# Layer 0 of a four-layer convolution network: the output scales as a row on every partition, made by a matrix product

## The chip, the cores and the metric

The kernel runs on one core of a Trainium2 chip. The time is the device time of one execution in microseconds (us). The kernel before took 5655.76 us, the median of three runs (5650.31, 5659.83 and 5655.76). The engines of the core are named as the profile names them: PE (matrix products; PEld is its weight load), DVE (VectorE), ACT (ScalarE), POOL (GpSimd) and SP, whose queue issues the transfers (DMA).

## What is computed

Input x has 32 images of 96 channels and 56 x 56 points. Four layers follow one another, each with a group normalisation in front and a sum with its input behind. Layer 0 is an inverted bottleneck with 576 inner channels:

```python
def _bn(x, g, b, m, v):
    scale = g / jnp.sqrt(v + EPS)                     # EPS = 0.001
    return x * scale[:, None, None] + (b - m * scale)[:, None, None]
identity = x
h = jnp.einsum('nchw,oc->nohw', x, w_exp)             # 96 -> 576
h = jax.nn.silu(_bn(h, g1, b1, m1, v1))
h = depthwise_3x3(h, w_dw)
h = jax.nn.silu(_bn(h, g2, b2, m2, v2))
s = h.mean(axis=(2, 3))
s = jax.nn.silu(s @ w_se1.T + b_se1)
s = jax.nn.sigmoid(s @ w_se2.T + b_se2)
h = h * s[:, :, None, None]
h = jnp.einsum('nchw,oc->nohw', h, w_proj)            # 576 -> 96
h = _bn(h, g3, b3, m3, v3)
return h + identity
```

(`depthwise_3x3` stands for the reference's grouped convolution.) Layer 1 is a wavelet convolution, layer 2 a quantised bottleneck, layer 3 a 9 x 9 depthwise convolution with kernels computed from `diff_metric`. Only the last normalisation of layer 0, with g3 and v3, is touched here: its 96 scales are folded into the projection weights.

## The kernel before

Layer 0 holds channels on partitions and takes one image after another. The order of the PE, DVE and ACT instructions of an image is written out by hand in `L0_ORDER`; the steps of image 0 up to its normalised input are in `FIRST = "s u m q v w b n"` and run ahead, outside the pipeline: s sums the image on ACT, u averages over channel groups on PE, m makes the mean on DVE, q and v do the same for squares, w (`deviation`, L393 and L395) makes the deviation on DVE and its power -1/2 on POOL, b (`norm_bias`, L399 to L403) the bias on DVE, n (`normalise`, L408) writes `xn` on ACT. Everything that PE does in layer 0 starts from `xn`.

Ahead of `FIRST` stand loads and small work on weights, whose order is the scheduler's:

- SP issues all loads in one queue (L278, L88, L268 and so on). The image comes first.
- `wproj` (128 partitions x 5 blocks x 96 outputs) is multiplied by the 96 output scales, which must lie as a row on each of the 128 partitions (L296 to L302). They are computed there: g3 and v3 are loaded as rows to all partitions (`out_rows`, at first room inside `h2s[0]`), POOL adds EPS (L299) and raises 128 x 96 values to -1/2 (L300), DVE multiplies by g3 (L301) and multiplies `wproj` by the row (L302).
- The scales of the other two normalisations (`sc`, `bi`, L315 to L328) have channels on partitions: POOL raises 128 x 5 and 128 x 11 values (L321). `both3` (`sc3`, `bi3`, L329 to L335) holds the same 96 output scales a second time, as a column: one value on each of 96 partitions (L332).
- `filt` (L344) spreads the depthwise taps over 32 x 32 unit matrices `eye4`, 3072 values on each partition, by one DVE multiplication. PE uses it as the weights of `psd` (L493).
- `brief` hands out short-lived room inside `h2s[1]`.

After `FIRST` the call `tables` makes the filter tables of layers 1 and 3: `diffusion_kernels` (L1385 to L1406; two powers of 96 x 81 values on POOL, L1402 and L1403, held back until the deviation of image 0 is issued), `wavelet_filters` (L643 to L694; small DVE work and many DVE copies into `zt`, L693) and `diffusion_filters` (L1415 to L1425; POOL copies `rev` and `zt`, then the transfer `zdiff`). Behind `tables` the pool `l0l` takes over the memory of the tables; it holds `hc`, `wg`, `hab` and one `h2` image. So `hc` (first written at L460 by ACT) has to wait until the tables are stored, `zdiff` last. The depthwise taps that run on DVE are L467 (`tap`), each reading the padded image and its own sum, both in SBUF.

`psum` of layer 0 has three buffers of the tag `mm`, taken in turn by all products of the expansion, filter and projection.

Of the kernel before, what the change touches and what calls it, by code (L numbers as in the profile page):

```python
# [10 lines left out]
F32 = mybir.dt.float32  # L11
# [4 lines left out]
ALU = mybir.AluOpType  # L16
# [4 lines left out]
B, C, H, W = 32, 96, 56, 56  # L21
# [19 lines left out]
EPS_L0 = 1e-3  # L41
# [199 lines left out]
def layer0(ctx, tc, S, x, w, y0, tables, aside, keep):  # L241
# [10 lines left out]
    nc = tc.nc  # L252
# [3 lines left out]
    psum = ctx.enter_context(tc.tile_pool(name="l0p", bufs=3, space=PSUM))  # L256
# [5 lines left out]
    ND = NBLK  # L262
    GC = 32
    HALF = 64

    def load(name, shape):
        t = cp.tile(shape, F32, tag=name, name=name)
        nc.sync.dma_start(t, w[name])  # L268
        return t
# [22 lines left out]
    wproj = load("l0_wproj", [128, ND, C])  # L292
    out4 = load("l0_out", [C, 4])

    h2s = [cp.tile([128, H, W], F32, tag=f"h2{i}", name=f"h2{i}") for i in range(2)]
    out_rows = h2s[0].rearrange("p h w -> p (h w)")[:, : 2 * C].rearrange("p (n c) -> p n c", n=2)  # L296
    nc.sync.dma_start(out_rows, w["l0_out_rows"].to_broadcast([128, 2, C]))
    gain = out_rows[:, 1]
    nc.gpsimd.tensor_scalar(gain, gain, EPS_L0, None, ALU.add)  # L299
    nc.gpsimd.tensor_tensor(gain, gain, S.mhalf[:, 0:1].to_broadcast([128, C]), ALU.pow)  # L300
    nc.vector.tensor_tensor(gain, gain, out_rows[:, 0], ALU.mult)  # L301
    nc.vector.tensor_tensor(wproj, wproj, gain.unsqueeze(1).to_broadcast([128, ND, C]), ALU.mult)  # L302
    room, at = h2s[1].rearrange("p h w -> p (h w)"), [0]

    def brief(*shape):

        n = math.prod(shape)
        at[0] += n
        t = room[:, at[0] - n : at[0]]
        return t if len(shape) == 1 else t.rearrange("p (a b) -> p a b", b=shape[1])  # L310
# [5 lines left out]
    for j in range(2):  # L316
        g, b_, m, v = ((mid1, mid2)[j][:, i, :] for i in range(4))
        n = (DV + NG, ND)[j]
# [3 lines left out]
        s = cp.tile([128, n], F32, tag=f"s{j}", name=f"s{j}")  # L322
# [7 lines left out]
    sc3, bi3 = both3[:, 0:1], both3[:, 1:2]  # L330
# [8 lines left out]
    planes = [cp.tile([128, HH, W2], F32, tag=f"plane{g}", name=f"plane{g}") for g in range(NG)]  # L339
    mv_all = cp.tile([C, B, 2], F32, tag="mv0", name="mv0")  # L340

    eye4 = brief(GC)
    nc.sync.dma_start(eye4, w["eye4"])
    nc.vector.tensor_tensor(filt, eye4.unsqueeze(1).to_broadcast([128, NG * NM, GC]),  # L344
                            wphase.rearrange("p g n -> p (g n)").unsqueeze(2).to_broadcast([128, NG * NM, GC]), ALU.mult)

# [2 lines left out]
    def image(b):  # L349

        if b not in ims:
            pair, xt = xs.pop(b)
            ims[b] = {
                "b": b, "pair": pair, "xt": xt, "h2": [None] * DV, "ps": [None] * NP, "pad": hpad, "added": set(),
                "ss": sm.tile([128, ND], F32, tag="ss", name="ss"),
            }
        return ims[b]


    small = psm.tile([128, 8, 8], F32, tag="small", name="small")  # L360
    pn = psm.tile([128, 2, B], F32, tag="pn", name="pn")
    spare = pairs[0].rearrange("c r i q -> c (r i q)")
    stats = spare[:, 3 * B : 3 * B + 12 * NP].rearrange("c (a b) -> c a b", b=6)
    later = []
# [245 lines left out]

    with tc.manual_schedule(engines=MANUAL):
        for s in FIRST.split():
            step[s](image(0))
    tables(ims[0]["pow"].ins)
    late = ctx.enter_context(tc.tile_pool(name="l0l", bufs=1))
# [895 lines left out]
def kernel_body(tc, w, x, out):  # L1511
    nc = tc.nc
    with ExitStack() as ctx:
# [29 lines left out]
        def keep():  # L1543
            pool = ctx.enter_context(tc.tile_pool(name="kept", bufs=1, side="right"))
            row = pool.tile([128, 2 * B + 1], F32, tag="row", name="row")
            return pool.tile([128, H * NPH, 2, W4], F32, tag="kept", name="kept"), row

        kept, row, left, made = layer0(tc, S, x, w, y0, tables,
               [lambda c=c: wavelet_matrices(nc, z1, z2, z3, t1, t2, t3, c) for c in range(C)]
               + [lambda c=c: matrix_rows(nc, td[c], zd[c], 1) for c in range(C)], keep)  # L1550
# [54 lines left out]
def layouts(a):  # L1605
# [25 lines left out]
    def halved(v):  # L1631

        c = v[256:320]
        return np.stack([v[:128], v[128:256], np.concatenate([c, c]), v[320:448], v[448:]], axis=1)
# [5 lines left out]
    def phase_taps(v):  # L1640
# [15 lines left out]
    i0, i2 = "L0_conv_", "L2_conv_"  # L1656
# [11 lines left out]
        "l0_wse1": halved(a[i0 + "w_se1"].T),  # L1668
        "l0_bse1": a[i0 + "b_se1"].reshape(SEH, 1),
        "l0_wproj": halved(a[i0 + "w_proj"].T),  # L1670
        "l0_out_rows": np.stack([a[i0 + "g3"], a[i0 + "v3"]])[None],
        "l0_out": np.stack([a[i0 + n] for n in ("g3", "b3", "m3", "v3")], axis=1),
        "l1_base": np.concatenate(
            [np.pad(a["L1_conv_base_w"].reshape(C, 5, 5)[:, ::-1], ((0, 0), (1, 1), (1, 1))).reshape(C, 49),
# [43 lines left out]
```

## Time and profile before

The profiled execution took 5647.33 us; the span of its instructions, to which all times of the trace refer, is 5645.5 us, so 1.8 us lie around it.

| what | value |
|---|---|
| median of three runs | 5655.76 us |
| profiled execution | 5647.33 us |
| its span | 5645.5 us |
| mean granted PE clock | 0.987 |
| PE, DVE, ACT, POOL busy from 0 to 24 us | 0.62, 0.62, 9.24, 16.56 us |
| the same from 24 to 44 us | 0.34, 5.53, 0.00, 15.51 us |
| the same from 44 to 101 us | 39.79, 48.43, 33.32, 49.51 us |
| PE busy from 242 to 800 us | 558.00 of 558 us |

The page gives busy time by engine, 40 slices of the span with a digit for each, and the chain of waits: the work that ended last, followed back from its end, each step to what released it. The timeline gives each instruction with its start and its length. An instruction's length can reach past the start of the next one on its engine; the distance between two starts is what it costs the queue.

### The profile page before, as it was taken

To read this page: it belongs to the slowest core of one execution; us is meant where nothing else is said; L and a number is where in the kernel's file an instruction comes from. 1 tells how busy PE (TensorE), PEld (TensorE's weight loads), DVE (VectorE), ACT (ScalarE), POOL (GpSimd) and SP (SyncE) were. 2 spreads that over 40 slices of the span, in tenths; PEclk is the share of its full clock that TensorE was granted. 3 is DMA by queue.
4 is the path that set the end of the run, shared out by engine and by line. 5 is a ranking of instruction groups with operands and counts; after the bars stand their busy time and mean duration, and the time that the engine had idled before them with its cause. 6 is when DMAs were issued, how large, how long until landed. Compare 5 with 4: busy or idle time off the path is not lost.

```text
span 5645.5 us, 137543 instructions
## 1 busy us (share of the span) xinstructions
PE 5420.9 (96%) x59704; PEld 3086.1 (55%) x59704; DVE 4691.7 (83%) x5413; ACT 4179.3 (74%) x6072; POOL 240.3 (4%) x161
## 2 busy tenths in 40 slices
PE   5999999999999999998899999999999999999999
PEld 2333333333333333333666666788878777787444
DVE  6999999999999999997777776777777777676777
ACT  5888888888888888885666664777777777676455
POOL 6000000000000000000000000000000000000000
PEclk9999999999999999998999999999999999999999
DMA  3023333322233232214577776479688697763888
GB/s 100 15 56 64 58 59 56 59 46 52 54 60 62 55 56 53 49 32 38 151 156 160 160 161 128 21 51 54 44 53 46 49 53 41 49 51 41 240 249 249
DMA packets 1289849, 456.13 MB, mean 81 GB/s; under 512 B 1104211, under 2 KB 1285187, under 8 KB 1287323
## 3 DMA queue, kind: packets, MB, share of 16 engines
q1 hardware_dynamic: 1289243, 447.32, 51.1%
q8 instruction: 469, 7.68, 0.6%
q14 instruction: 137, 1.12, 0.1%
HBM read 285.41 MB, written 214.08 MB: 88 GB/s over the span
## 4 chain that ended last, share of the span: by engine, by line
PE 82%; ACT 5%; DVE 5%; DMA 4%; issue 2%; SPq 1%; POOL 1%; ACTq 0%; DVEq 0%; POOLq 0%
PE psd L493 18%; PE psd L1294 13%; PE psj L548 11%; PE ps L426 8%; PE ps L1275 7%; PE pse L449 6%; PE pc L935 5%; PE pc L1469 4%; PE psj L1337 4%; DMA X<-y 2%; ACT hi L1245 2%; PE pc L923 1%; PE pa L897 1%; ACT u L1265 1%; DVE xl L884 1%
## 5 line engine op out<-in xcount | busy, mean ns | idle before, releaser
L467 DVE SCALAR_TENSOR_TENSOR h<-hpad,l_wdw,h 128x3136 f32<-128x3136 f32 x512 | 1782.2, 3481 | 9.1
L493 PE MATMUL psd<-plane,filt 128*32 128x392 f32 (+5 forms) x16384 | 1084.1, 485 | 0.6 <-issue 0.6
L1294 PE MATMUL psd<-apad,diag 64*64 64x392 bf16 x20736 | 914.5, 330 | 54.0 <-issue 50.1
L1294 PEld LDWEIGHTS <-diag 64*64 64x64 bf16 x20736 | 700.9, 106 | 262.8 <-issue 97.0
L493 PEld LDWEIGHTS psd<-plane,filt 128*32 128x32 f32 (+1 forms) x16384 | 389.5, 108 | 676.3 <-issue 623.5
L1265 ACT ACTIVATE u<-ps,o,s 128x784 int16<-128x784 f32 x576 | 537.4, 1003 | 164.9 <-PE ps L1275 145.9
L1265 ACT ACTIVATE a<-psd,o,s 128x784 int16<-128x784 f32 x448 | 424.6, 1002 | 263.3 <-PE psd L1294 263.2
L748 ACT COPY T<-raw 128x112 f32<-128x112 f32 (+2 forms) x1386 | 445.9, 385 | 230.0 <-DMA raw<-tdiff 170.3
L426 PE MATMUL ps<-xn,l_wboth 96*128 96x392 f32 (+1 forms) x1536 | 465.9, 506 | 23.9 <-ACT xn L408 23.2
L467 DVE SCALAR_TENSOR_TENSOR hc<-hhalf,l_wdw,hc 128x1568 f32<-128x1568 f32 x256 | 473.7, 1850 | 16.2 <-ACT hc L460 9.5
L1275 PE MATMUL ps<-hi,l_w1q 96*128 96x392 f32 x1280 | 464.0, 363 | 6.7 <-DVE u L1263 3.8
L935 PE MATMUL pc<-x,T 128*112 128x416 f32 (+1 forms) x1152 | 451.6, 529 | 6.1 <-DVE x L873 6.1
L1275 PE MATMUL ps<-lo,l_w1q 96*128 96x392 f32 x1280 | 439.2, 343 | 2.9 <-DVE lo L1253 2.9
L1469 PE MATMUL pc<-x,T 128*112 128x416 f32 (+1 forms) x1152 | 417.1, 523 | 13.8 <-ACT T L748 7.7
L449 PE MATMUL pse<-xn,l_wboth 96*32 96x392 f32 x4096 | 392.3, 501 | 4.5 <-ACT hab L470 4.5
L426 PEld LDWEIGHTS ps<-xn,l_wboth 96*128 96x128 f32 (+1 forms) x1536 | 219.4, 173 | 249.2 <-issue 54.5
L470 ACT ACTIVATE hab<-psd,o,s 128x784 f32<-128x784 f32 x256 | 283.7, 1113 | 59.5 <-PE psd L493 57.3
L1469 PEld LDWEIGHTS pc<-x,T 128*112 128x112 f32 x1152 | 203.2, 177 | 227.2 <-issue 188.7
L436 ACT ACTIVATE hpad<-ps,o,s 128x784 f32<-128x784 f32 x256 | 278.5, 1104 | 50.1 <-PE ps L426 48.8
L548 PE MATMUL psj<-h,wg 128*32 128x392 f32 x3072 | 306.4, 514 | 0.1
L548 PE MATMUL psj<-hab,wg 128*32 128x392 f32 x3072 | 304.8, 510 | 0.0
L935 PEld LDWEIGHTS pc<-x,T 128*112 128x112 f32 x1152 | 193.6, 180 | 154.9 <-issue 154.9
(267 smaller groups left out, 7684.8 us busy)
## 6 DMA issues: line engine op xcount, KB each, us to landing
X<-y SPq DMA_DIRECT2D x192, 392.0 KB
y<-xt SPq DMA_DIRECT2D x108, 392.0 KB
y<-y SPq DMA_DIRECT2D x96, 392.0 KB
out_dram<-y SPq DMA_DIRECT2D x96, 392.0 KB
twav<-zwav SPq DMA_DIRECT2D x768, 36.8 KB
y<-kept SPq DMA_DIRECT2D x72, 392.0 KB
xt<-y SPq DMA_DIRECT2D x59, 392.0 KB
xt<-in_x_dram SPq DMA_DIRECT2D x8, 2352.0 KB
```

The costliest lines, as they stand in the source:

```text
L426: nc.tensor.matmul(ps[p, j, :NT], wexp[:, k * 128 : k * 128 + 128][:, m], im["xn"][:, j, rows, :].rearrange("c h w -> c (h w)"), start=Tru ...
L449: nc.tensor.matmul(ps[f * GC : (f + 1) * GC, half, :NT].rearrange("p (r w) -> p r w", w=W2), wexp[:, c : c + GC], im["xn"][:, f % 2, r0 : ...
L467: nc.vector.scalar_tensor_tensor(h2, taken(im, k, t), wdw[:, k, t : t + 1], h2, ALU.mult, ALU.add)
L470: nc.scalar.activation(view, ps, AF.Silu, bias=bi[1][:, c : c + 1], scale=sc[1][:, c : c + 1], accum_out=accum)
L493: nc.tensor.matmul(ps[at * GC : (at + 1) * GC, r, :NT].rearrange("p (r w) -> p r w", w=W2)[:, r0 - half * n : r1 - half * n, q0:q1], filt[ ...
L548: nc.tensor.matmul(ps[s * GC : (s + 1) * GC, t, :NT].rearrange("c (m r q) -> c r q m", m=2, q=W4), wg[p, k, c * GC : (c + 1) * GC], phases ...
L748: nc.scalar.copy(to.rearrange("x t (p s) -> x t p s", p=NPH), v[:, k])
L935: nc.tensor.matmul(ps[:PH, to], st["T"][j][:, h, k, :], st["x"][:, j, h, of], start=first and n == 0, stop=not first and n == NK - 1)
L1265: nc.scalar.activation(out, ps, AF.Identity, bias=o[:, c : c + 1], scale=s[:, c : c + 1])
L1275: nc.tensor.matmul(ps[:, j, :NT], w1[:, k * 128 : k * 128 + 128], im[part][:, r0 : r0 + RT, :].rearrange("c h w -> c (h w)"), start=(part ...
L1294: nc.tensor.matmul(ps[q, j, :NT].rearrange("p (r w) -> p r w", w=W), diag[p, k, t, :], v, start=(t == 0), stop=(t == 8))
L1469: nc.tensor.matmul(ps[:, :, to], st["T"][:, h, k, :], st["x"][:, h, :, of], start=(n == 0), stop=(n == NK - 1))
```

## The change

The row of scales is no longer computed on 128 partitions. It is made out of the column `sc3`, which the kernel computes anyway: `each3` is `sc3` copied along 128 columns (96 x 128), `eye3` is a 96 x 96 unit matrix put together from `eye4`, and the product of the two on PE has the 96 scales as a row on each of 128 partitions. DVE multiplies `wproj` by it out of PSUM. That product and the multiplication are called between the steps b and n of `FIRST`.

```diff
-    out_rows = h2s[0].rearrange("p h w -> p (h w)")[:, : 2 * C].rearrange("p (n c) -> p n c", n=2)
-    nc.sync.dma_start(out_rows, w["l0_out_rows"].to_broadcast([128, 2, C]))
-    gain = out_rows[:, 1]
-    nc.gpsimd.tensor_scalar(gain, gain, EPS_L0, None, ALU.add)
-    nc.gpsimd.tensor_tensor(gain, gain, S.mhalf[:, 0:1].to_broadcast([128, C]), ALU.pow)
-    nc.vector.tensor_tensor(gain, gain, out_rows[:, 0], ALU.mult)
-    nc.vector.tensor_tensor(wproj, wproj, gain.unsqueeze(1).to_broadcast([128, ND, C]), ALU.mult)
...
-    eye4 = brief(GC)
+    eye4, eye3, each3 = brief(GC), brief(C)[:C], brief(128)[:C]
     nc.sync.dma_start(eye4, w["eye4"])
+    nc.vector.memset(eye3, 0.0)
+    for i in range(C // GC):
+        at = slice(i * GC, (i + 1) * GC)
+        nc.vector.tensor_copy(eye3[at, at], eye4[at])
+    nc.vector.tensor_copy(each3, sc3.to_broadcast([C, 128]))
     nc.vector.tensor_tensor(filt, eye4.unsqueeze(1).to_broadcast([128, NG * NM, GC]),
...
+    def scaled_weights():
+        gain = psum.tile([128, 2, 512], F32, tag="mm", name="psg")[:, 0, :C]
+        nc.tensor.matmul(gain, each3, eye3, start=True, stop=True)
+        nc.vector.tensor_tensor(wproj, wproj, gain.unsqueeze(1).to_broadcast([128, ND, C]), ALU.mult)
...
         for s in FIRST.split():
+            if s == "n":
+                scaled_weights()
             step[s](image(0))
...
-        "l0_out_rows": np.stack([a[i0 + "g3"], a[i0 + "v3"]])[None],
```

## Prediction

> **What bounds the kernel now.** I read the page's busy table and slices first, then the chain of waits for the first 110 us, then the timelines of DVE and POOL there.
>
> ```profile
> PE 5420.9 (96%) x59704; PEld 3086.1 (55%) x59704; DVE 4691.7 (83%) x5413; ACT 4179.3 (74%) x6072; POOL 240.3 (4%) x161
> PE   5999999999999999998899999999999999999999
> POOL 6000000000000000000000000000000000000000
> ```
>
> PE fills nearly every slice of 141 us but the first, and the first is the only one in which POOL works for long. So the kernel as a whole is PE's; what this change can touch is how late PE gets going. The chain says what that hangs on (start, length, what):
>
> ```profile
> 15.49 3.37 DMA h<-in_l_out_rows_dram
> 18.93 0.47 POOL h L299
> 19.59 0.23 POOL h L320
> 19.82 1.17 POOL h L321
> 20.99 15.61 POOL h L300
> 36.60 2.08 POOL h L321
> 38.69 0.51 POOL both L332
> 39.20 4.45 issue
> 43.68 0.56 POOL rstd L395
> ...
> 89.02 6.32 POOL zt L1424 x16
> 95.35 5.78 DMA zdiff<-zt
> 101.24 1.61 ACT hc L460
> ```
>
> The power of the row, L300, lies on the chain with 15.6 us; the small powers that everybody needs queue behind it. What the chain calls issue is filled in by the timeline:
>
> ```profile
> 38.88 0.65 DVE L302 TENSOR_TENSOR l_wproj<-l_wproj,h 128x480 f32<-128x480 f32 x1
> 39.75 3.35 DVE L344 TENSOR_TENSOR filt<-h 128x3072 f32<-128x3072 f32 x1
> 43.09 0.15 DVE L384 TENSOR_REDUCE ts<-small 96x1 f32<-96x4 f32 x1
> 44.45 3.98 ACT L408 ACTIVATE xn<-xt,nb,rstd 96x784 f32<-96x784 f32 x4 [20.65 <-DVE nb L399]
> ```
>
> PE's second group sum, which L384 waits for, is done by 24.3 us: nothing but DVE's queue (the multiplication of wproj and filt, held by POOL's powers) keeps xn from starting. From the deviation (rstd, 43.68) on, POOL goes through the tables until 95.35, zdiff is stored until 101.2, and hc, PE's filters and the pipeline follow. From 242 to 800 us PE is busy for 558 of 558 us: a shift of its start should reach the end.
>
> **The change, part by part.** Costs in a queue are distances between starts.
>
> *The load of out_rows (96 KB) goes.* SP issues one every 0.47 us, so the loads behind it, mid1, wphase, eye4 and the tables', go out 0.47 us earlier. POOL waited for out_rows until 18.93; in the changed order it waits next for mid1 (22 KB), issued in that place at 15.49. Not later than 18.93, then; earlier by at most the 74 KB less at the 110 GB/s that flowed there (0.67 us). I take 18.6.
>
> *POOL.* L299 (0.43) and L300 (15.60) go. Left are the sums on mid1 (0.24) and sc3 (0.19), then the powers of 5 columns (1.18), 11 (2.08) and 1 (0.55): 18.6 + 0.43 = 19.03, 20.21, 22.29, 22.84. Before, the last ended at 39.20. The row costs 0.16 us a column, the same in L300 (96 columns, 15.64) and L1402 (81 columns, 13.80). Here the Trainium skill speaks against the change: GPSIMD Engine Reference, § 4.1 Engine selection, has POOL about twice as slow as DVE in two-input elementwise work. DVE multiplies the same 128 x 96 values in 0.26 us (L301), so by the rule L300 would be 0.5 us and the change would bring nothing. The row decides: this operation is a power, and the trace has it at thirty times the rule's price.
>
> *DVE ahead of filt.* L301 goes (beside POOL, on no path of its own); L302 leaves this place (0.57). After both3 at 22.9 the order has six small ones at 0.075 (0.45), three copies of 32 x 32 (unseen; by the copies of 96 x 25 into G at 0.08 to 0.09: 0.27; bounds 0.2 and 0.5) and the copy to 96 x 128 (unseen; between the 96 x 81 and 96 x 162 rows, 0.11 and 0.23: 0.2). filt starts at 23.85. The memset of eye3 comes first in DVE's queue, which is idle until 19.1: nothing; without that cover some 0.2. eye4 and wphase have long landed, as DMA is idle from 21 us on.
>
> *From filt to xn.* filt still holds the queue for 3.27 us: L384 at 27.1. That is what is late next; PE's sum has lain ready since 24.3. Then 0.52 (0.59 less L335, which no longer stands between) to the power of the deviation at 27.65, and 0.77 as before to xn at **28.4 in place of 44.45: 16.0 us earlier**.
>
> *The product psg.* Its weights and its 96 x 96 stream are like the group sums' (0.4 and 0.3 us) and fall into PE's idle time between 24.3 and 31. If that cover were gone, 0.7 us.
>
> *wproj out of PSUM* stands behind b1 and ahead of the diffusion chain's z in DVE's queue. Price 0.57 as L302: PSUM adds nothing, since L567 with one PSUM input takes 555 ns for 392 values and L302 652 ns for 480. Waiting behind it: the z chain, hence POOL's table powers, and the zt copies. They are **15.5 us earlier, not 16.0**. psg takes one of three mm buffers, so the third pair of expansion products waits for this multiplication; that is over near 29.5, and PE needs the buffer 2.6 us after its first product, near 34.
>
> *POOL's tables.* Do they keep pace? Each copy to rev lies in one of two classes:
>
> ```profile
> L1415 POOL COPY rev<-yy x9: 187/189/3649, 75.2 to 86.2; 96x9 f32<-96x9 f32 x9
> 75.72 14.03 DVE L467 SCALAR_TENSOR_TENSOR h<-hpad,l_wdw,h 128x3136 f32<-128x3136 f32 x4
> 89.92 3.48 DVE L467 SCALAR_TENSOR_TENSOR h<-hpad,l_wdw,h 128x3136 f32<-128x3136 f32 x1
> ```
>
> Median 189 ns, but up to 3649: as long as a DVE tap. A copy is held until the tap beside it ends. The same page of the skill (§ 8 Key points) has POOL contending with DVE instructions that read two SBUF inputs, which the taps do. So POOL's end follows DVE's last tap (93.4) and some ten free copies of 0.2, and what counts is whether DVE's taps keep pace. In the changed order the first two taps stand a little ahead of the third set of filter sums. The first waits for ACT's h, which ends at 60.46 - 16.0 = 44.4, and DVE gets there at about 44.25. That wait is 0.2 us, DVE's work is the same, and the tables move by 15.5. Lower bound of the shift 14.5 (a few copies held again), upper 16.5.
>
> *Behind it.* zdiff, then hc at 85.7 in place of 101.24. PE's gap before its filters (4.46 us at 106.7) grows by the half us that xn gained more. PE's granted clock was 0.50 from 105.3 to 112.2 there. The skill (TensorE: Matmul & The Clock Gate, Part 1) lets the clock fall and rise by windows of about 3.4 us that don't start with the kernel. By the row I would copy the half-speed time unchanged; by the rule it may differ by a window, 1.7 us of time either way. I take the row, the rule widens the range.
>
> **Sum.** -15.5 us (-13 to -17.5). Against the profiled execution: 5647.33 - 15.5 = 5631.8. That execution was 8.4 us below the median of the three runs; from the median, **5640.3**.
>
> **Rivals.**
>
> *The gain is taken back later (5655.8).* A transfer or table chain that doesn't start with xn would have to set layer 0's end. For it: the loads at the start do have fixed times, and DVE is 97% busy in layer 0 (541.5 of 558 us). Against: DMA share is 0.00 from 24 to 44 us, so all loads are in, and the later transfers stand in SP's queue behind zwav and zdiff, which move too. DVE's taps also begin earlier.
>
> *Slower.* One place: DVE's first tap, now ahead of the third set of filter sums. DVE takes its queue in order, so a wait W there delays the zt copies, the later taps, POOL's held copies, zdiff and hc by W. It decides from W = 15.5 and shows as slower from W = 26.8 (5667). The timeline gives ACT's h at 60.46, one us before the tap of the old place; W near 27 would need h behind all of ACT's expansions, and it is ACT's fifth piece of work after the table load.
>
> That the change doesn't do what it says is out: the new order has no power of 96 columns, and PE's and ACT's orders differ by psg alone.
>
> **How the numbers follow.** The forecast has 0.82, the gain taken back 0.13, slower 0.05. The forecast's own range is 5634 to 5647: the shift's bounds and the runs' scatter of 4 to 5 us about the median. A measurement of this kernel can tell about 0.2%, 11.3 us, from no change; 15.5 is not far beyond it, and about one in eight of the first case would read as the same. So faster 0.72; same 0.10 + 0.13 = 0.23; slower 0.05. The range reaches towards the second case: 5632 to 5652.
>
> **What would show it.** POOL without L300 and its last small power ending near 22.8; filt starting near 23.9 and xn near 28.4; psg in PE's idle time; the zdiff transfer issued near 79.8 (95.35 before) and hc near 85.7; from there the same rows, 15.5 us earlier, to a span near 5630. Wrong if xn starts early but hc stays where it was (POOL or zdiff bound by something else), if hc moves but the span doesn't, or if the first tap waits for many us.

## Result and profile after

The kernel after took 5639.6 us (median of 14 runs, 5626.5 to 5656.4), the kernel before, on the same chip, 5652.3 us (median of 14 runs, 5642.3 to 5666.6): a ratio of 0.9973, 95% interval 0.9963 to 0.9983. The profiled execution took 5626.9 us, its span 5625.0 us against 5645.5.

The page of the kernel after, busy table and slices:

```profile
PE 5413.7 (96%) x59706; PEld 3072.7 (55%) x59706; DVE 4693.5 (83%) x5417; ACT 4177.4 (74%) x6072; POOL 226.9 (4%) x159
PE   6999999999999999998899998999999999999999
POOL 5000000000000000000000000000000000000000
```

PE's first slice rises from 5 to 6 tenths and POOL's falls from 6 to 5: apart from one late slice of PE that reads 8 for 9, these two rows differ in the first 141 us alone. The chain of waits of the kernel after, first 110 us (start, length, what):

```profile
15.39 2.19 DMA h<-in_l_mid_dram
17.66 0.26 POOL h L313
...
18.10 3.26 POOL h L314 x2
21.36 0.51 POOL both L325
21.88 4.94 issue
26.85 0.56 POOL rstd L399
...
43.40 16.70 POOL z L1409
60.17 2.75 POOL z L1411
63.00 3.36 POOL yy L1412
66.43 10.83 POOL rev L1421 x9
...
79.87 2.54 POOL zt L1430 x16
82.43 5.77 DMA zdiff<-zt
88.38 1.61 ACT hc L464
```

The 15.6 us of the row's power are gone and the small powers end at 21.88 (39.20 before). The deviation comes at 26.85 (43.68), and `xn` starts at 27.62 in place of 44.45: 16.83 us earlier. But `hc` starts at 88.38 in place of 101.24: 12.86 us earlier. Some 4 us were lost in between, and they sit on this chain as POOL's work on the tables. The rows of the same three operations, first from the POOL timeline of the kernel before, then of the kernel after (start, length, line):

```profile
60.29 13.31 POOL L1403 TENSOR_TENSOR z<-z,yy 96x81 f32<-96x81 f32 x1
73.69 1.01 POOL L1405 TENSOR_SCALAR z<-z 96x81 f32<-96x81 f32 x1
74.79 0.35 POOL L1406 TENSOR_TENSOR yy<-z,yy 96x81 f32<-96x81 f32 x1
```

```profile
43.40 16.68 POOL L1409 TENSOR_TENSOR z<-z,yy 96x81 f32<-96x81 f32 x1
60.17 2.74 POOL L1411 TENSOR_SCALAR z<-z 96x81 f32<-96x81 f32 x1
63.00 3.36 POOL L1412 TENSOR_TENSOR yy<-z,yy 96x81 f32<-96x81 f32 x1
```

The second table power took 3.37 us longer, the two small operations behind it 1.73 and 3.01 us. What stood beside them is in the DVE timeline of the kernel after:

```profile
43.44 3.47 DVE L471 SCALAR_TENSOR_TENSOR h<-hpad,l_wdw,h 128x3136 f32<-128x3136 f32 x1
...
59.16 14.03 DVE L471 SCALAR_TENSOR_TENSOR h<-hpad,l_wdw,h 128x3136 f32<-128x3136 f32 x4
...
73.36 3.47 DVE L471 SCALAR_TENSOR_TENSOR h<-hpad,l_wdw,h 128x3136 f32<-128x3136 f32 x1
90.01 3.74 DVE L471 SCALAR_TENSOR_TENSOR hc<-hhalf,l_wdw,hc 128x1568 f32<-128x1568 f32 x2 [13.19 <-ACT hc L464]
```

The first depthwise tap of image 0, which in this order stands ahead of the third set of filter sums, starts at 43.44: 0.04 us after the second power. Before, it started at 61.53, 1.24 us after it. The power grew by about one tap's length. Follow the advance over the kernel before along POOL: 16.9 us where the second power starts, 13.5 behind it, 11.8 and 8.8 behind the two small operations, 9.2 at the copies into `zt`. Those copies then take 2.53 us and not 6.31, because DVE's last tap is over at 76.8 and they run beside nothing: 12.9 at the store of `zdiff`. DVE itself sits idle for 13.19 us until `hc` comes.

### The profile page after: what moved, and what is told of

Read it like the earlier page. It is cut to its first block, busy times and chain, and to the rows that moved or that the text cites. A ratio compares the mean times of both kernels' runs of the same rounds, so it can differ in the third digit from the quotient of the medians.

```text
span 5625.0 us, 137545 instructions
## 1 busy us (share of the span) xinstructions
PE 5413.7 (96%) x59706; PEld 3072.7 (55%) x59706; DVE 4693.5 (83%) x5417; ACT 4177.4 (74%) x6072; POOL 226.9 (4%) x159
## 4 chain that ended last, share of the span: by engine, by line
PE 76%; DMA 8%; ACT 6%; DVE 5%; SPq 2%; issue 2%; POOL 1%; ACTq 0%; DVEq 0%; POOLq 0%
PE psd L497 18%; PE psd L1300 13%; PE psj L552 11%; PE ps L430 8%; PE ps L1281 7%; PE pse L453 6%; PE pc L941 4%; PE psj L1343 3%; DMA X<-y 3%; ACT hi L1251 2%; ACT u L1271 2%; PE pc L1475 1%; PE pc L929 1%; DMA raw<-tdiff 1%; DVE h L471 1%
## 5 line engine op out<-in xcount | busy, mean ns | idle before, releaser
L471 DVE SCALAR_TENSOR_TENSOR hc<-hhalf,l_wdw,hc 128x1568 f32<-128x1568 f32 x256 | 473.7, 1850 | 19.9 <-ACT hc L464 13.2
L1475 PE MATMUL pc<-x,T 128*112 128x416 f32 (+1 forms) x1152 | 418.6, 524 | 14.0 <-ACT T L754 11.8
```

The source lines that it names most:

```text
L471: nc.vector.scalar_tensor_tensor(h2, taken(im, k, t), wdw[:, k, t : t + 1], h2, ALU.mult, ALU.add)
L1475: nc.tensor.matmul(ps[:, :, to], st["T"][:, h, k, :], st["x"][:, h, :, of], start=(n == 0), stop=(n == NK - 1))
```

## Experiments

The theory after this reading: the early `xn` is worth about 16.5 us, and the tap's new place gives some 4 back, since a POOL instruction that starts beside a tap is held until the tap ends. Rivals: the gain comes from less work, so that a row power moved elsewhere on POOL would cost its 16 us still; the lost 4 us belong to something other than the tap's place. Each of the first four kernels ran beside the same kernel before (median of 67 runs 5649.5 us), the last three beside another set (median of 46 runs 5647.7 us).

**The power put back, with its result unused.** The kernel after, plus the load, EPS and the power of 96 columns in their old places; the scales still come from the product.

```diff
+    out_rows = h2s[0].rearrange("p h w -> p (h w)")[:, : 2 * C].rearrange("p (n c) -> p n c", n=2)
+    nc.sync.dma_start(out_rows, w["l0_out_rows"].to_broadcast([128, 2, C]))
+    gain = out_rows[:, 1]
+    nc.gpsimd.tensor_scalar(gain, gain, EPS_L0, None, ALU.add)
+    nc.gpsimd.tensor_tensor(gain, gain, S.mhalf[:, 0:1].to_broadcast([128, C]), ALU.pow)
```

> The changed kernel, with the load of the rows, their EPS and their power of 128 x 96 on GpSimd put back in the old place; their result is not used, the scales still come from the product. Theory (the power stands in GpSimd's queue ahead of the small powers, and all else hangs on those): the normalised input of image 0 starts near 44.4 us again, hc near 101 to 104, ratio to the kernel before 1.000 within 0.001. Rival (the gain comes from what else changed: VectorE's two multiplications ahead of filt, their order, the product on the idle TensorE): the normalised input stays below 30 us and the ratio near 0.997.

Measured: 5649.5 us, ratio 0.9999 (0.9985 to 1.0012). `xn` starts at 44.5, as expected, and `hc` at 105.2, beyond the expected 101 to 104. POOL timeline of this kernel, then a row of its DVE timeline:

```profile
20.62 15.63 POOL L300 TENSOR_TENSOR h<-h,mhalf 128x96 f32<-128x96 f32 x1
...
60.32 16.68 POOL L1414 TENSOR_TENSOR z<-z,yy 96x81 f32<-96x81 f32 x1
```

```profile
60.36 3.47 DVE L476 SCALAR_TENSOR_TENSOR h<-hpad,l_wdw,h 128x3136 f32<-128x3136 f32 x1
```

The whole gain goes with work on POOL whose result nobody reads: `xn` is 16.9 us later than in the kernel after, 15.6 of them the power and 1.3 the load and the EPS sum that came back with it. And the run isolates the loss: `xn` stands where it stood before, the second power starts where it started before (60.32 against 60.29), but takes 16.68 us, with the first tap at 60.36; `hc` is 4.0 us later than before. That is the price of the new order alone. The 16.8 us of early `xn` less these 4.0 make the 12.9 of the kernel after, to within 0.1 us.

**The power kept, but late.** The kernel before, with the row's power behind image 1's deviation on POOL, and `wproj` multiplied where image 0's gated weights are made; no product.

```diff
+        if im["b"] == 1:
+            with tc.issue_after(im["pow"].ins):
+                nc.gpsimd.tensor_scalar(wg[:, 1], wg[:, 1], EPS_L0, None, ALU.add)
+                nc.gpsimd.tensor_tensor(wg[:, 1], wg[:, 1], S.mhalf[:, 0:1].to_broadcast([128, C]), ALU.pow)
...
+        if im["b"] == 0:
+            nc.vector.tensor_tensor(wg[:, 1], wg[:, 1], wg[:, 0], ALU.mult)
+            nc.vector.tensor_tensor(wproj, wproj, wg[:, 1].unsqueeze(1).to_broadcast([128, ND, C]), ALU.mult)
```

> The kernel before, with the row still made by GpSimd's power of 128 x 96, but issued behind the deviation of image 1, and multiplied into wproj just ahead of the first gated weights; no product on TensorE. Theory (only the place in GpSimd's queue mattered): normalised input near 26.9 us, hc near 85, layer 0 some 16 us ahead, ratio 0.997. Rival (the power has to be removed, since GpSimd's 16 us come back as a wait of image 1 or of the first projection): the normalised input as early, but layer 0 by its end less than 6 us ahead, ratio above 0.999.

Measured: 5630.8 us, ratio 0.9974 (0.9964 to 0.9984); `xn` at 27.1, `hc` at 84.0. POOL timeline of this kernel:

```profile
42.48 13.29 POOL L1404 TENSOR_TENSOR z<-z,yy 96x81 f32<-96x81 f32 x1
...
104.41 18.82 POOL L392 TENSOR_TENSOR wg<-wg,mhalf 128x96 f32<-128x96 f32 x1
```

The power is even longer here, 18.82 us beside DVE's taps (it starts 0.17 us behind the start of one, at 104.24), and costs the kernel nothing: it ends at 123.2, and its result is read at 140.8. So it was never the amount of POOL's work, only its place ahead of the small powers: the first rival is out. The old order of the taps leaves the second power at 13.29 us, and `hc` gains 17.3, all that `xn` gained.

**The first tap behind the third filter set.** The kernel after, with one order mended on DVE (`MARK["g"]` is the last copy into `G`).

```diff
+        if "g" in MARK:
+            with tc.issue_after(MARK.pop("g").ins):
+                nc.vector.scalar_tensor_tensor(h2, taken(im, k, t), wdw[:, k, t : t + 1], h2, ALU.mult, ALU.add)
+            return
...
-                nc.vector.tensor_copy(g, F[:, abs(da), abs(dp)])
+                MARK["g"] = nc.vector.tensor_copy(g, F[:, abs(da), abs(dp)])
```

> The changed kernel, with VectorE's first depthwise tap put behind the third set of filter sums again, as in the kernel before. Theory (in the changed kernel the tap started 0.04 us after the second table power and held it for its whole length): the second power takes 13.3 us in place of 16.7, GpSimd's tables end near 79 us in place of 82.4, hc starts near 85 in place of 88.4, the end some 3.4 us earlier than the changed kernel's. Rival (the tables are held by taps in any order because the taps came forward by more than the tables): second power or the pieces behind it held as long, tables end within 1 us of 82.4.

Measured: 5629.7 us, ratio 0.997 (0.996 to 0.998). POOL timeline of this kernel, then the first tap from its DVE timeline:

```profile
43.66 13.29 POOL L1416 TENSOR_TENSOR z<-z,yy 96x81 f32<-96x81 f32 x1
57.04 1.51 POOL L1418 TENSOR_SCALAR z<-z 96x81 f32<-96x81 f32 x1
58.63 0.35 POOL L1419 TENSOR_TENSOR yy<-z,yy 96x81 f32<-96x81 f32 x1
```

```profile
45.36 3.47 DVE L476 SCALAR_TENSOR_TENSOR h<-hpad,l_wdw,h 128x3136 f32<-128x3136 f32 x1
```

The tap starts at 45.36, 1.7 us after the power, and the power is whole again at 13.29 us, though this tap and the next run wholly within it. `hc` starts at 85.2, 16.1 us earlier than before and 3.2 earlier than in the kernel after: with one order mended the tables move by about what was forecast (15.5). The second rival is out too.

**`filt` taken off the path to `xn`.** The kernel after, with the multiplication of `filt` behind image 0's bias (`BEHIND[0]` is the instruction that makes `b1`).

```diff
+    with tc.issue_after(BEHIND[0].ins):
+        nc.vector.tensor_tensor(filt, eye4.unsqueeze(1).to_broadcast([128, NG * NM, GC]),
```

> The changed kernel, with the multiplication that makes filt put behind the bias of image 0 in VectorE's order. Theory (filt's 3.3 us is what stands ahead of the deviation once the power is gone, until TensorE's sum at 24.3): normalised input near 25.1 us in place of 27.6, hc at least 2 us earlier than 88.4. Rival (something else is late as well, the loads or GpSimd's small powers): normalised input within 0.5 us of 27.6.

Measured: 5631.8 us, ratio 0.9973 (0.9963 to 0.9984). `xn` at 26.8, 0.8 earlier than in the kernel after and not the 2.5 expected: the step that reads PE's second group sum comes at 25.58, behind fourteen short table operations that took `filt`'s place in DVE's queue. The miss has a use. The diffusion chain was among them, so both powers ran back to back (26.81 and 40.07), unheld at 13.29 and 13.27 us, 3.9 us ahead of the first tap at 43.94. But then the first small operation behind them met DVE's memset and third tap (POOL timeline):

```profile
53.42 5.10 POOL L1414 TENSOR_SCALAR yy<-yy 96x81 f32<-96x81 f32 x1
```

It takes 0.5 us when free and ended 0.3 us after that tap. The copies into `rev` took 14.32 us (10.84 in the kernel after). `hc` starts at 85.6: at least 2 us earlier than in the kernel after, as expected, but no earlier than in the run before it (85.2). Powers that are done earlier only reach the taps earlier.

**The tables' tail on DVE.** The kernel after, with the three small operations, the nine copies into `rev`, the memset and the sixteen copies into `zt` of the diffusion tables issued on DVE, behind the third set's last copy.

```diff
+                with tc.issue_after(LAST["copy"].ins):
+                    diffusion_filters(nc, tp, *kernels, zd, room)
...
-        nc.gpsimd.tensor_copy(rev[:, KS - 1 - ky], kern[:, KS * ky : KS * ky + KS])
+        nc.vector.tensor_copy(rev[:, KS - 1 - ky], kern[:, KS * ky : KS * ky + KS])
...
-            nc.gpsimd.tensor_copy(Z[:, pi, lo : lo + KS, po, valid[0] : valid[-1] + 1], rev[:, :, kx::NPH])
+            nc.vector.tensor_copy(Z[:, pi, lo : lo + KS, po, valid[0] : valid[-1] + 1], rev[:, :, kx::NPH])
```

> The changed kernel with the three small operations behind the table powers, the nine reversed rows, the memset and the sixteen copies of the diffusion tables moved from GpSimd to VectorE. Theory (GpSimd's small operations are held by the taps, and the late tables hold hc): the first tap still starts just before the second power, so that one stays at 16.7 us and ends near 60.2; VectorE, which has done three taps and the third filter set by 59.2, then does the tail between two more taps and ends it near 74; the tables' store is issued near 74.3 (82.43 in the changed kernel) and hc starts near 80 (88.38). VectorE now carries about 7 us more ahead of its first hc tap and has only 13.19 us of idle time there, so the hc tap comes at about 84.7 (90.01), and layer 0 is 5 us earlier than in the changed kernel: some 18.5 to 19 earlier than before. Time 5632 to 5636 by the changed kernel's 5639.6, ratio to before 0.996 to 0.997. Rival (the tables are not what holds layer 0, VectorE's work is): 7 us more work on VectorE makes layer 0 7 us later than in the changed kernel, some 7 earlier than before, ratio 0.9985.

Measured: 5634.3 us, in the expected 5632 to 5636, ratio 0.9978 (0.9966 to 0.9991), a little above the expected 0.996 to 0.997. POOL's second power and DVE's first tap, each from its timeline:

```profile
43.02 13.26 POOL L1412 TENSOR_TENSOR z<-z,yy 96x81 f32<-96x81 f32 x1
```

```profile
43.84 3.47 DVE L474 SCALAR_TENSOR_TENSOR h<-hpad,l_wdw,h 128x3136 f32<-128x3136 f32 x1
```

With no small operation between the two powers, the second power starts at 43.02 and the tap at 43.84: a lead of 0.82 us was enough to leave it unheld (13.26 us), which I had not expected. The store is issued at 71.8. `hc` did not follow: it starts at 83.2, not 80. The ACT timeline shows why, and the DVE timeline what it led to:

```profile
78.99 0.95 ACT L381 ACTIVATE unread<-xt,nm 96x784 fp8e4<-96x784 f32 x1 [16.68 <-DVE nm L396]
...
83.16 1.59 ACT L467 ACTIVATE hc<-hhalf,l_wdw 128x1568 f32<-128x1568 f32 x1
```

```profile
84.78 3.74 DVE L474 SCALAR_TENSOR_TENSOR hc<-hhalf,l_wdw,hc 128x1568 f32<-128x1568 f32 x2 [2.50 <-ACT hc L467]
```

ACT makes the squares of image 1 ahead of `hc`, and these wait for image 1's mean, which DVE reaches at 78.74, behind its taps. So with the tables out of the way the bound is DVE's queue, and the first tap of `hc` comes at 84.78 (expected 84.7; 90.01 in the kernel after). DVE's idle time there falls from 13.19 to 2.50 us. The rival, by which every microsecond more on DVE makes layer 0 later, is out: DVE carries more, and `hc` is 5.2 us earlier.

**All of it together.** The tail on DVE, `filt` later and the first tap behind the third set: the edits of the last three kernels in one.

> The kernel of the tail on VectorE, with the filter spread behind image 0's bias and the first tap behind the third filter set as well. Theory: both table powers run unheld, 13.3 us each, from about 26.8 to 53.4; VectorE starts on the tail behind its third tap and the third set's copies, at about 59.5, waits for nothing, and ends it near 73; store near 73.5, hc near 79, first hc tap near 84, the same VectorE work as with the tail alone, so that it is VectorE's order that sets it now. Layer 0 is 19 to 20 us earlier than before, about 1 more than with the tail alone, and 3 more than with the first tap behind the third set alone (16.6). Ratio to before 0.996 to 0.997. Rival (the rest of the shift is lost somewhere else, as in the run with the filter spread later, where nothing was gained beyond 16.5): 16 to 17 us here too.

Measured: 5629.9 us, ratio 0.9967 (0.9956 to 0.9978). Both powers unheld, done at 53.3; `hc` at 83.5 (expected near 79), its first tap at 85.14 (expected near 84). Nothing is gained over the tail alone in layer 0, where about 1 us was expected: DVE's tail begins 0.35 us later (59.76 against 59.41), and `hc` is later by as much.

**The kernel after once more.** No edit.

> The changed kernel itself, unaltered, on the same chip as the two runs with the tail on VectorE and beside the same runs of before. Every theory: ratio to before 0.997 within 0.001, and layer 0 13.7 us earlier than before within 0.5, with xn near 27.6 and hc near 88.4; where layer 0 differs by more than 0.5 from its first profile, differences of a few us between the other runs' layer 0 are not to be read either.

Measured: 5640.7 us, ratio 0.9985 (0.9971 to 0.9999), not 0.997 within 0.001 as expected; span 5639.0 us. `xn` at 28.2 and `hc` at 88.9, each 0.5 to 0.6 later than in the first profile: the load that POOL starts on landed at 18.20 and not 17.66. But the advance over the kernel before late in layer 0 is 11.3 us, not 13.7, so the expected 0.5 was missed. The windows from 88 to 110 us hold a part of it, first in the first profile, then in this one (busy PE, PEld, DVE, ACT and POOL, granted PE clock, DMA share, GB/s):

```profile
88.00:110.00 22.00, 16.14 (x216) 5.58 (x220) 19.37 (x12) 15.24 (x16) 3.75 (x1) 0.84 0.57 132
```

```profile
88.00:110.00 22.00, 15.60 (x176) 5.08 (x176) 18.83 (x12) 14.68 (x15) 3.75 (x1) 0.77 0.55 132
```

Where PE takes up its filters it was granted 0.84 of its clock in one execution and 0.77 in the other. How much that is worth can be read from PE's own rows. The same 16 products `pse` and 256 products `psd` follow there without a pause; their rows are from the PE timelines of the kernel before, of the first profile of the kernel after and of this one:

```profile
106.72 2.84 PE L449 MATMUL pse<-xn,l_wboth 96*32 96x392 f32 x16 [4.46 <-ACT hab L470]
109.34 18.23 PE L493 MATMUL psd<-plane,filt 128*32 128x392 f32 x256
```

```profile
93.86 2.84 PE L453 MATMUL pse<-xn,l_wboth 96*32 96x392 f32 x16 [7.32 <-ACT hab L474]
96.48 17.24 PE L497 MATMUL psd<-plane,filt 128*32 128x392 f32 x256
```

```profile
94.40 2.84 PE L453 MATMUL pse<-xn,l_wboth 96*32 96x392 f32 x16 [7.57 <-ACT hab L474]
97.02 18.69 PE L497 MATMUL psd<-plane,filt 128*32 128x392 f32 x256
```

In windows of 0.1 us the granted clock is 0.50 from 105.5 to 112.3 us in the kernel before, from 90.7 to 97.5 in the first profile and from 90.7 to 100.9 in this one.

| profile | first start to last end | length | of it at clock 0.50 | half of that and the rest |
|---|---|---|---|---|
| before | 106.72 to 127.57 | 20.85 | 5.59 | 18.06 |
| after | 93.86 to 113.72 | 19.86 | 3.61 | 18.05 |
| after once more | 94.40 to 115.71 | 21.31 | 6.51 | 18.06 |

With each microsecond at clock 0.50 counted as half, the three lengths are equal to 0.01 us: in this stretch the clock is the whole difference. Of the 2.4 us between the two profiles late in layer 0 it makes 1.45, and 0.54 were there at `hc`. So I read the kernels at `hc`, which repeats within 0.5 us, and do not read differences of 2 us later in layer 0.

The kernels side by side; "late in layer 0" is the start of the last deviation on POOL between 1800 and 2100 us, against the kernel before (2044.25):

| kernel | `xn` | 2nd power | `hc` | late in layer 0 | span | median, ratio |
|---|---|---|---|---|---|---|
| before | 44.45 | 13.31 | 101.2 | 0 | 5645.5 | 1 |
| after | 27.6 | 16.68 | 88.4 | -13.7 | 5625.0 | 5639.6, 0.9973 |
| after once more | 28.2 | 16.68 | 88.9 | -11.3 | 5639.0 | 5640.7, 0.9985 |
| power back, unused | 44.5 | 16.68 | 105.2 | +4.1 | 5640.6 | 5649.5, 0.9999 |
| power late | 27.1 | 13.29 | 84.0 | -16.4 | 5623.9 | 5630.8, 0.9974 |
| tap behind third set | 27.9 | 13.29 | 85.2 | -16.7 | 5619.0 | 5629.7, 0.9970 |
| `filt` later | 26.8 | 13.27 | 85.6 | -15.9 | 5642.4 | 5631.8, 0.9973 |
| tail on DVE | 27.9 | 13.26 | 83.2 | -18.2 | 5622.1 | 5634.3, 0.9978 |
| all together | 26.8 | 13.27 | 83.5 | -18.0 | 5627.8 | 5629.9, 0.9967 |

Five versions start `hc` 3 to 5 us earlier than the kernel after, and their medians are 5 to 11 us lower than its two (13.4 to 19.9 us below the kernel before that ran beside them, against 12.7 and 7.0). But 3 to 5 us are under 0.1%, and the intervals overlap: that they beat the change is likely from their traces, not shown by the times.

## Why the prediction was right, and where it was not

- **What bounds.** Right, and shown by two runs: the power put back takes the gain away; the power moved late gives all of it without the product. POOL's queue ahead of the small powers held `xn`.
- **The load.** Right in kind, low in size. POOL starts on `mid` at 17.66 (forecast 18.6; 17.63 to 18.20 in the kernels without the row). The limit of 0.67 us that I drew from the load's bytes was too tight: it was 1.27. The 110 GB/s behind it are what the trace of before has on average over its first 120 us; in the half-microsecond windows of the wait itself the rate went from 56 to 269.
- **POOL's small powers.** 3.26 us for 5 and 11 columns, 0.51 for one: as reckoned. They end 0.96 earlier than forecast (21.88 for 22.84), nearly all of it the load's.
- **The skill's rule against the row.** The row was right. POOL took 15.63 us for 128 x 96 powers in the run that put them back.
- **DVE ahead of `filt`.** The three 32 x 32 copies cost 0.55 us between starts, not 0.27, and fall outside the upper bound of 0.5; the copy to 96 x 128 cost 0.14, not 0.2. `filt` starts at 23.12 for 23.85.
- **From `filt` to `xn`.** 3.27, 0.46 and 0.77 us for 3.27, 0.52 and 0.77. `xn` at 27.62 for 28.4.
- **The product, and `wproj` out of PSUM.** The product ran from 24.11 to 24.83 in PE's idle time; the multiplication kept DVE's queue for 0.57 us, as L302 had. It held the z chain as forecast: the first table power starts 16.43 us earlier than before, 0.40 less than `xn`. That does not show behind it, because the first power took 13.30 us (29.43) where it had taken 13.80 (45.86). The 13.80 that I used as a price was itself half a microsecond too long; what made it so the record does not show.
- **The tables: the term that was mis-sized.** "That wait is 0.2 us, DVE's work is the same, and the tables move by 15.5." They moved by 12.9. I had looked at the tap's new place for a wait on DVE, found almost none, and concluded that nothing else could happen there. The tap did run at once, and by that it met the start of POOL's second power and held it for 3.37 us. I had applied the rule that a tap holds POOL to the copies of 0.2 us only, though my own numbers had the two side by side: 15.5 us earlier, the second power would start at 44.8, and I had the tap at 44.4. The second error stands beside it: "POOL's end follows DVE's last tap". It did so before; once POOL was thrown back, it ended 5.6 us after the last tap (82.4 against 76.8). My lower bound of 14.5 did not reach it. The run with power back prices the step at 4.0 us, the run with the tap behind the third set gives 3.2 of it back.
- **Behind the tables, and PE's clock.** PE's gap before its filters grew from 4.46 to 7.32 us and not by half a microsecond, since `hc` came later than forecast. By the row I copied the half-speed time unchanged; by the rule of the Trainium skill (TensorE: Matmul & The Clock Gate, Part 1) I let it differ by a window, which I estimated at 1.7 us. The rule was nearer. The half-speed stretch lasted 6.8 us before and in the first profile after, and 10.2 us in the second, two, two and three times the rule's 3.4 us, and the filters met 5.59, 3.61 and 6.51 us of it. By half of these stretches the clock gave the first profile 1.0 us beyond what `hc` had gained, and took 0.5 from the second.
- **The shift reaches the end.** Through layer 0 it does (13.7 us late in it, and 11.3 in the second profile). Behind it the profiles part: from there to the end of the span the kernel after gains another 6.8 us in one execution and loses 4.8 in the other. One kernel differs that much from itself there, so neither figure can be laid to the change.
- **The time.** 5640.3 was forecast and 5639.6 came, closer than its working deserves. The kernel before ran at 5652.3 in that comparison, not at 5655.8, so the change was 12.7 us there and 7.0 in the repeat, not 15.5.

The first rival (taken back later) fell: the loads were all in, and `hc` moved with the tables. The second (slower, by the first tap's place) had the right place and the wrong effect: not a wait of DVE that grows to 27 us, but a hold on POOL of 3 to 4.

## What to carry over

Ask of a long instruction on a small engine first what queues behind it: this one cost 16 us ahead of three short powers, of 11, 1 and 1 columns, and nothing behind them. When a change reorders another engine's queue, set the new starts against the starts of the long instructions they contend with; a fraction of a microsecond decided here whether a power of 13.3 us took 16.7. And where the end scatters more than the effect, compare marks within the stage (here `xn` and `hc`) before comparing spans.

## What the runs showed of the hardware

- A POOL power of 96 x 81 values was held at its start only. With the first tap 0.04 or 0.05 us behind its start it took 16.68 us, in three profiles; with the tap 0.82, 1.24, 1.7, 3.9 or 5.5 us behind, it took 13.26 to 13.31, with whole taps inside it. The power of 128 x 96 that was moved late agrees: it started inside a tap with 3.3 us to go, and took 18.82 us in place of 15.63 though taps ran beside it to its end. The taps themselves kept their 3.47 us either way. Where between 0.04 and 0.82 us the limit lies was not tried.
- A short POOL operation that reads SBUF and meets a tap ends 0.2 to 0.3 us after the tap, whether 0.7 or 2.5 us of the tap were left: 73.69 + 1.01 = 74.70 in the kernel before, with the tap over at 74.43; 60.17 + 2.74 = 62.91 in the kernel after, with the tap over at about 62.6. A POOL memset, which reads nothing, was not held: `zt` took 2.61 us wholly inside a tap (86.34 in the kernel before) and 2.61 us with no tap beside it (77.19 in the kernel after). In the kernel with `filt` later one started beside DVE's memset, at 53.42, and did not end in the 1.45 us before the next tap either, though it takes 0.5 alone; that DVE's memset holds POOL too is suggested by this one row, not shown.
- Two profiles of the same kernel had spans of 5625.0 and 5639.0 us, with layer 0 only 2.5 us apart.
